# A float32 fast-multiplication kernel: turns for two engines in its planner, finer products as single steps, and two more products split

## Chip, cores and metric

One core of one Trainium2 chip. The metric is device time in microseconds (us), the median of several runs. Five engines matter: PE multiplies, DVE (VectorE) and POOL (GpSimd) add and subtract, ACT (ScalarE) copies, SP (SyncE) starts the transfers.

## What is computed

`x` is 64 sequences of 64 tokens with 1024 features, so 4096 tokens, all float32. Two residual layers follow each other. The first adds a low-rank product chosen by a sequence's adapter. The second adds a full 1024 x 1024 product and a mixture of eight low-rank experts, of which the two best by a router count, with a bias for the sequence's language.

```python
def _L0_cond_ref(x, A, B, adapter_ids):
    B_req = B[adapter_ids]
    A_req = A[adapter_ids]
    Bx = jnp.einsum('bni,bri->bnr', x, B_req)
    out = jnp.einsum('bnr,bor->bno', Bx, A_req)
    return out * SCALING
...
def _L1_cond_ref(x, language_ids, W, Wr, A, B):
    base = jnp.einsum('btd,od->bto', x, W)
    logits = jnp.einsum('btd,ed->bte', x.astype(jnp.float32), Wr.astype(jnp.float32))
    ...
    topw, topi = jax.lax.top_k(logits, TOP_K)
    weights = jax.nn.softmax(topw, axis=-1)
    gates = jnp.sum(jax.nn.one_hot(topi, E, dtype=weights.dtype) * weights[..., None], axis=-2)
    h = jnp.einsum('btd,erd->bter', x, A)
    lora_out = jnp.einsum('bter,bte,eor->bto', h, gates, B)
    return base + SCALING * lora_out
...
x = x + _L0_cond_ref(x, L0_cond_A, L0_cond_B, itok_B_4_50)
x = x + _L1_cond_ref(x, itok_B_0_7, L1_cond_W, L1_cond_Wr, L1_cond_A, L1_cond_B)
```

## The kernel before

**Tiling.** Tokens come in eight blocks of 512, held with features on the partitions. Two blocks make a stage `s`, so there are four stages, s = 0 to 3. The identity is added to the diagonal of W, so that the large product gives the residual too.

**Three levels of fast multiplication.** The large product of a stage is done with seven half-size products in place of eight (the outer level, `n`, in the order 1, 2, 6, 7, 5, 3, 4), and each of these with seven inner products (`k`, in the same order) in place of eight. An inner product is four matmuls of 128 x 128 weights with 256 tokens. From s = 1 (FINE, line 256) some inner products are split once more: `fine_product` (line 995) makes them of seven matmuls of 128 x 128 with 128 tokens. `fine_of` (line 669) says which: k = 2 for every n, and k = 4 for the n in FOURTH (line 257), except in the last product of the kernel. The last stage's last n keeps k = 2 alone.

**What a split product needs.** Sums of weight blocks (`fine_weights`, line 746): made in stage 1 by four instructions on POOL in one step, stored in `f_kept`, loaded again in stages 2 and 3. Sums of token blocks (`begin_fine`, line 979): three instructions on POOL in one step into a "tt" tile. Its matmuls go in four parts (`fine_product`, parts 0 to 3), one after each of the following whole products (`advance`, line 1163). After each of the first three parts ACT copies some of the sums in PSUM into a "cp" tile. After the last, DVE adds PSUM to the output (`leave`, line 951), and then `rest_` (line 1057) adds the copied pieces on POOL by three instructions in one step.

**Other work.** `turn`, `project` and `adapt` (lines 418 to 507) do the first layer for a block; `rows`, `gates` and `weigh` (lines 509 to 623) do the router. `inner_tokens` (line 800) makes four token sums for each n ("ti" tiles), on DVE in stage 0 and on POOL afterwards. `weights` (line 709) makes inner weight sums on POOL in stage 0, stores them in `s_kept`, and later loads seven of them for each n. `outer` and `token_sum` make the outer level's sums on DVE. A matmul of the gated rows with the expert weights ("extra", two for each product) joins the products with n and k in (2, 7, 3, 4).

**Who sets the order.** Every piece of work is a step given to `Plan` (line 34): engines that may do it with a cost in us, what it reads and writes, a due time `at`, buffers that it takes, and `sb` when all its operands lie in SBUF. `order` (line 65) walks through time: among the steps that could start soonest on an engine (within LOOK, 0.2 us) it takes the one with the earliest due time. If a DVE step and a POOL step with `sb` overlap, both are stretched by PACE (lines 145 to 152). The outcome is each engine's own list in program order (`Pinned`, line 19). On the chip every engine runs its list and waits for data and buffers alone.

**Buffers** (line 263). PSUM has two banks for "a" (pa, products 1, 6, 5, 3), two for "b" (pb, products 2, 7, 4 and the split k = 2) and four for "l", shared by turns, projections, rows and the split k = 4. An adaptation takes four "l" at a time (line 475). In SBUF "s" holds 27 tiles of weights, "tt" and "cp" three each.

In the profile all instructions issued through `Pinned` carry line 29, so one goes by the names: pf is a split product, tt its token sums, sf its weight sums, cp the copied pieces, u, v and o the sums that become the output, px an adaptation, pt and pg transposes, ph rows.

Of the kernel before, what the change touches and what calls it, by code (L numbers as in the profile page):

```python
# [33 lines left out]
class Plan:  # L34
# [14 lines left out]
    AHEAD = 6.0  # L49
    PACE = {"DVE": 0.36, "POOL": 0.73}  # L50
    SET = {"SP": 1.2, "DVE": 3.1, "POOL": 2.9}
# [13 lines left out]
    def order(self):  # L65
# [34 lines left out]
        turn = {tag: 0 for tag in turns}  # L100
        clock, end, where, now = dict(self.SET), {}, {}, {}
        moved = 0.0
        done = []
# [78 lines left out]
def kernel(  # L182
# [73 lines left out]
    FINE = 1  # L256
    FOURTH = (1, 2, 6, 7, 3)

# [212 lines left out]
    def adapt(k, h, at):  # L471
# [33 lines left out]
        for gi in range(NG):  # L505
            xs = part(x, gs=[gi])
            plan.add({"DVE": 0.62}, out(gi), [(px[gi],)] + xs, xs, at - 2 + 1.5 * gi * (k == 0))

# [157 lines left out]
    s_kept = tc.dram_tile([7, 7, P, QC * QO], F32, name="s_kept")  # L666
    f_kept = tc.dram_tile([7, 2, P, QC * QO], F32, name="f_kept")
# [16 lines left out]

    DVE = {"DVE": 0.62}
    POOL = {"POOL": 1.25}

    def outer(n, at):

        if n == 5:  # L690
            m_q[5] = {k: ("m5",) + k for k in quarter[1, 0]}
            for k in m_q[5]:
                combine(m_q[5][k], quarter[1, 0][k], quarter[1, 1][k], ALU.add, at, DVE)
        elif n == 7:
            m_q[7] = quarter[1, 0]
            for k in m_q[7]:
                combine(m_q[7][k], quarter[0, 0][k], m_q[7][k], ALU.subtract, at, DVE)
        elif n == 6:
            m_q[6] = quarter[0, 0]
            for k in m_q[6]:  # L700
                combine(m_q[6][k], m_q[5][k], m_q[6][k], ALU.subtract, at, DVE)
        elif n == 3:
            m_q[3] = quarter[0, 1]
            for k in m_q[3]:
                combine(m_q[3][k], m_q[3][k], m_q[6][k], ALU.subtract, at, DVE)

    wt, ti = {}, {}

    def weights(s, n, at):
# [17 lines left out]
        for k, (u, v, op) in {  # L727
# [7 lines left out]
            vv = m[v] if isinstance(v, tuple) else out[v]  # L735
            combine(out[k], uu, vv, op, at - 4, POOL)
        for k in ORDER:
# [8 lines left out]
    def fine_weights(s, n, k, a, at):  # L746

        t, kept = ("sf", s, n, k), f_kept[n - 1, k // 4]

        def blocks():  # L750
            made[t] = new("s", [P, QC, QO], f"sf_{s}_{n}{k}")
            return made[t].rearrange("p c (o w) -> p (c o) w", w=P)

# [3 lines left out]

        def sums(e):
            f, w4 = blocks(), made[a].rearrange("p c (o w) -> p (c o) w", w=P)
            a11, a21, a12, a22 = (w4[:, x] for x in range(4))  # L760
            v = engine[e]
            v.tensor_tensor(f[:, 0], a21, a22, ALU.add)
            v.tensor_tensor(f[:, 1], f[:, 0], a11, ALU.subtract)
            v.tensor_tensor(f[:, 2], a11, a21, ALU.subtract)
            v.tensor_tensor(f[:, 3], a12, f[:, 1], ALU.subtract)

# [3 lines left out]
        if s == FINE:  # L770
            plan.add({"POOL": 1.6}, sums, [(a,)], [(t,)], at - 3, [("s", t)], sb=True)
            plan.add({"SP": 0.1}, keep, [(t,)], [("fine", n, k)], at + 4, kb=256)
        else:
            plan.add({"SP": 0.1}, load, [("fine", n, k)], [(t,)], at - 6, [("s", t)], kb=256)
        wt[n]["fine", k] = t
# [24 lines left out]
    def inner_tokens(s, n, m, at):  # L800
# [7 lines left out]
        for k, u, v in ((5, (0, 1), (0, 0)), (6, (1, 1), 5), (7, (1, 1), (0, 1)), (4, (1, 0), 6)):  # L808
            t = ("ti", s, n, k)

            def fn(e, t=t, k=k, u=u, v=v):
# [5 lines left out]
            plan.add(  # L817
                POOL if s else DVE, fn, keys(*u) + vk, [(t,)], at - 5,
                [(f"t{k}", t)], sb=True,
# [39 lines left out]
    def products(s):  # L859
# [91 lines left out]
        def leave(n, ps, i, cs, js, more=False):  # L951
# [18 lines left out]
            if d == n and not fresh:  # L970
                reads.append((name(d, i), 0, 0))
            plan.add(
                {"ACT": 0.6} if src is None else DVE, fn, reads, qk(d, i, cs, js), at() - 4,
                [("o", name(d, i))] * fresh,
# [4 lines left out]
        def begin_fine(n, k):  # L979

            t, (tx, tk) = ("tt", s, n, k), ti[n][k]

            def fn(e):
                made[t] = new("tt", [P, 4, P], f"tt_{s}_{n}{k}")
                f, b, v = made[t], tx(), engine[e]
                b11, b21 = b[:, 0, :P], b[:, 1, :P]
                v.tensor_tensor(
                    f[:, :2], b[:, :, P:], b[:, 0, :].rearrange("p (h t) -> p h t", t=P), ALU.subtract
                )
                v.tensor_tensor(f[:, 2], f[:, 1], b11, ALU.add)  # L990
                v.tensor_tensor(f[:, 3], b21, f[:, 2], ALU.subtract)

            plan.add({"POOL": 1.7}, fn, tk, [(t,)], at() - 3, [("tt", t)], sb=True)

        def fine_product(n, k, part_):


            ps, cp, tag = ("pf", s, n, k), ("cp", s, n, k), "b" if k == 2 else "l"
            a, f, t, (tx, tk) = wt[n][k], wt[n]["fine", k], ("tt", s, n, k), ti[n][k]
            extra = hd[n][k] if n in (2, 3, 7, 4) and part_ == 3 else None  # L1000
            oh, row = {2: 0, 3: 0, 7: 1, 4: 1}.get(n), k // 4

# [28 lines left out]

            reads = [(a,), (f,), (t,)] + tk + ([("b1",), extra[1]] if extra is not None else [])
            plan.add(
# [14 lines left out]
            if part_ < 3:  # L1048
# [4 lines left out]
                return  # L1053
            leave(n, ps, row, ALL, (0,), True)
            region = qk(dest[n], row, ALL, (0,))

            def rest_(e):
                o, c, v = q(dest[n], row, ALL, (0,)), made[cp], engine[e]
# [6 lines left out]
            done(n, row, ALL, (0,))  # L1065

# [62 lines left out]
        def step(n, k):  # L1129
# [8 lines left out]
            if k in (1, 6, 5, 3):  # L1138
# [5 lines left out]
                if k == 5 and last(n):  # L1144
                    leave(n, ps, 0, ALL, (1,))
                if k == 5 and 4 in fine_of(s, n):
                    leave(n, ("pb2", s, n), 1, ALL, (0,), True)
# [24 lines left out]
        for n in ORDER:  # L1172
# [21 lines left out]
            else:  # L1194
# [113 lines left out]
```

## Time and profile before

| | us |
|---|---|
| median of 3 runs | 516.18 (515.77 to 516.62) |
| the profiled execution | 517.08 |
| its span, first to last instruction | 515.3 |
| granted TensorE clock | 0.999 |
| first matmul starts, last one ends | 9.8, 511.7 |
| PE busy between 59 and 511 | 451.97 of 452 |
| DVE busy, 59 to 183 (stage 0) | 95.5 of 124 |
| DVE busy, 183 to 249, 249 to 307 | 39.2 of 66, 37.3 of 58 |
| POOL busy, 59 to 183 | 72.9 of 124 |
| POOL busy, 183 to 249, 249 to 307 | 55.9 of 66, 38.2 of 58 |
| mean transfer rate | 211 GB/s |

The span is the stretch that the trace covers; the execution's time also has what lies around it. Busy time of a stretch is read engine by engine; an engine that is idle and for which nobody waits costs nothing. A matmul in float32 leaves two records in the trace, each shown longer than the distance to the next one, since matmuls are pipelined.

### The profile page before, as it was taken

Reading aid. Unit: us, or ns where it says so; the run is one execution under the profiler, and the core shown is the slowest. Engines: PE = TensorE matmul, PEld = TensorE weight load, DVE = VectorE, ACT = ScalarE, POOL = GpSimd, SP = SyncE. Lnnn points to the kernel's source line nnn. Section 1 sums busy time; section 2 is a strip of 40 time slices with the busy share of each in tenths; the row PEclk is TensorE's granted clock in tenths of the full one; section 3 lists DMA queues with packets and bytes.
Section 4 is the critical chain, followed back from the end, with each engine's and each line's share of the span. In section 5 each row is a group of like instructions: output and inputs, shape, how many; then the busy total and the mean of one; then the engine's idle time right before and its main releaser. Section 6 shows DMA issues by size and latency. Waiting matters only on the chain.

```text
span 515.3 us, 9478 instructions
## 1 busy us (share of the span) xinstructions
PE 501.1 (97%) x3648; PEld 441.6 (86%) x3648; DVE 329.3 (64%) x589; ACT 71.4 (14%) x189; POOL 318.7 (62%) x405
## 2 busy tenths in 40 slices
PE   2999999999999999999999999999999999999997
PEld 2857988889889998899888999889889899998986
DVE  0689998987975275536985456463878526742833
ACT  1111100001001130012110121102301111111110
POOL 3063058095467686997958557972954755997811
PEclk9999999999999999999999999999999999999999
DMA  7999185799585303999577633981855754581023
GB/s 260 371 354 369 67 280 211 256 332 317 176 261 206 90 15 101 335 342 350 173 253 248 211 131 118 380 281 43 284 176 190 246 149 134 169 270 41 38 98 111
DMA packets 59452, 108.69 MB, mean 211 GB/s; under 512 B 5520, under 2 KB 11664, under 8 KB 59408
## 3 DMA queue, kind: packets, MB, share of 16 engines
q1 hardware_dynamic: 57104, 99.70, 56.7%
q0 software_dynamic: 2304, 8.39, 4.8%
q8 instruction: 29, 0.48, 0.4%
q14 instruction: 15, 0.12, 0.1%
HBM read 75.30 MB, written 32.77 MB: 210 GB/s over the span
## 4 chain that ended last, share of the span: by engine, by line
PE 97%; DMA 2%; DVE 0%; issue 0%; SPq 0%; POOL 0%
PE pa L29 39%; PE pb L29 23%; PE pf L29 15%; PE ph L29 12%; PE px L29 3%; PE pw L29 3%; DMA x<-in_xT 2%; PE pt L29 1%; PE pg L29 1%; DVE o L29 0%; SPq L29 0%; DVE bx L29 0%; POOL x L29 0%
## 5 line engine op out<-in xcount | busy, mean ns | idle before, releaser
L29 PE MATMUL pa<-ti,s 128*128 128x256 f32 x432 | 102.0, 380 | 0.0
L29 PEld LDWEIGHTS pa<-ti,s 128*128 128x128 f32 x432 | 79.2, 190 | 9.8 <-issue 0.2
L29 PE MATMUL pb<-ti,s 128*128 128x256 f32 x264 | 65.6, 380 | 0.0
L29 PE MATMUL ph<-a_sb,x 128*128 128x136 f32 x512 | 62.8, 279 | 0.2 <-issue 0.2
L29 PEld LDWEIGHTS ph<-a_sb,x 128*128 128x128 f32 x512 | 61.8, 190 | 1.1 <-issue 0.4
L29 ACT COPY cp<-pf 128x128 f32<-128x128 f32 (+1 forms) x108 | 32.2, 302 | 201.0 <-PE pf L29 189.1
L29 PEld LDWEIGHTS pb<-ti,s 128*128 128x128 f32 x264 | 48.6, 190 | 5.9
L29 PE MATMUL pa<-x,s 128*128 128x256 f32 x216 | 52.4, 380 | 0.0
L29 POOL TENSOR_TENSOR ti<-x,ti 128x512 f32<-128x512 f32 x24 | 32.2, 1340 | 27.7 <-PE pf L29 22.6
L29 POOL TENSOR_TENSOR o<-o,cp 128x128 f32<-128x128 f32 (+1 forms) x54 | 34.5, 651 | 20.9 <-DVE o L29 15.6
L29 DVE TENSOR_TENSOR x<-px,x 128x512 f32<-128x512 f32 x64 | 39.8, 683 | 10.8 <-PE px L29 10.7
L29 PEld LDWEIGHTS pa<-x,s 128*128 128x128 f32 x216 | 39.4, 190 | 4.9 <-issue 0.2
L29 PE MATMUL pf<-tt,sf 128*128 128x128 f32 x216 | 42.1, 278 | 0.0
L29 POOL TENSOR_TENSOR ti<-t 128x512 f32<-128x512 f32 x18 | 23.3, 1294 | 29.3 <-PE pa L29 16.8
L29 POOL TENSOR_TENSOR ti<-x 128x512 f32<-128x512 f32 x24 | 31.0, 1292 | 16.7 <-PE pb L29 11.2
L29 PE MATMUL pa<-t,s 128*128 128x256 f32 x168 | 41.2, 380 | 0.0
L29 PEld LDWEIGHTS pf<-tt,sf 128*128 128x128 f32 x216 | 35.5, 191 | 3.2 <-issue 0.8
L29 DVE TENSOR_TENSOR o<-pa,u 128x512 f32<-128x512 f32 x32 | 22.0, 687 | 22.2 <-PE pa L29 11.2
L29 POOL TENSOR_TENSOR s<-w,w 128x512 f32<-128x512 f32 x12 | 17.1, 1428 | 29.1 <-PE pa L29 13.2
L29 POOL TENSOR_TENSOR ti<-t,ti 128x512 f32<-128x512 f32 x18 | 25.3, 1404 | 15.7 <-PE pf L29 12.2
L29 PEld LDWEIGHTS pa<-t,s 128*128 128x128 f32 x168 | 30.8, 190 | 3.9 <-issue 0.2
L29 DVE TENSOR_TENSOR o<-pb,o 128x512 f32<-128x512 f32 x35 | 23.6, 688 | 8.7 <-ACT o L29 4.6
(150 smaller groups left out, 850.9 us busy)
## 6 DMA issues: line engine op xcount, KB each, us to landing
s<-s_kept SPq DMA_DIRECT2D x147, 256.0 KB, 3.9
x<-in_xT SPq DMA_DIRECT2D x15, 1024.0 KB, 6.8
out_T<-o SPq DMA_DIRECT2D x30, 512.0 KB, 3.2
s_kept<-s SPq DMA_DIRECT2D x28, 256.0 KB, 4.6
sf<-f_kept SPq DMA_DIRECT2D x24, 256.0 KB, 2.8
s_kept<-w SPq DMA_DIRECT2D x18, 256.0 KB, 5.6
w<-in_w SPq DMA_DIRECT2D x16, 256.0 KB, 7.5
f_kept<-sf SPq DMA_DIRECT2D x12, 256.0 KB, 3.3
```

The costliest lines, as they stand in the source:

```text
L29: return self._tc.keep_in_program_order(f(*args, **kwargs))
```

## The change

The planner's stretch by PACE goes. In its place, a step with `sb` may start only when the last one with `sb`, on either engine, has ended; among engines that could start at the same time the one that was ready first goes first. Costs of several steps are raised a little (0.62 to 0.65 or 0.69, 1.25 to 1.3). FOURTH now names all seven n. A split k = 4 begins after product 6 instead of after 7, and the old order of what is left over (3, then 4) remains only for the n without a split k = 4. The sums of split products become steps of one instruction that may go to DVE or to POOL: four for weights, three for tokens, and two in place of three for the copied pieces. "s" gets 26 tiles, `f_kept` a third row. A new tuple THIRD (products with k = 3 split) is empty, so its branches do nothing.

```diff
@@ class Plan
-    PACE = {"DVE": 0.36, "POOL": 0.73}
...
-            return t
+
+            return (max(t, shared_), t) if st["sb"] else (t, t)
...
-            t0 = min(can[e])[0]
-            _, n, t = min((steps[n]["at"], n, t) for t, n in can[e] if t <= t0 + self.LOOK)
+            t0 = min(can[e])[0][0]
+            _, n, t = min((steps[n]["at"], n, t) for (t, _), n in can[e] if t <= t0 + self.LOOK)
...
-            other = {"DVE": "POOL", "POOL": "DVE"}.get(e)
-            if st["sb"] and other in now and clock[other] > t and steps[now[other]]["sb"]:
-
-                mine, theirs = st["eng"][e] / self.PACE[e], (clock[other] - t) / self.PACE[other]
-                both = min(mine, theirs)
-                clock[e] = t + both + (mine - both) * self.PACE[e]
-                clock[other] = t + both + (theirs - both) * self.PACE[other]
-                end[now[other]] = clock[other]
-            now[e] = n
+            if st["sb"]:
+                shared_ = clock[e]
...
-    FOURTH = (1, 2, 6, 7, 3)
+    FOURTH = (1, 2, 6, 7, 5, 3, 4)
+    THIRD = ()
...
-        "q": 7, "s": 27, "tt": 3, "cp": 3, "t5": 2, "t6": 2, "t7": 2, "t4": 2, "o": 3, "hg": 3, "hd": 3,
+        "q": 7, "s": 26, "tt": 3, "cp": 3, "t5": 2, "t6": 2, "t7": 2, "t4": 2, "o": 3, "hg": 3, "hd": 3,
...
-        return ((2, 4) if n in FOURTH and (s, n) != (NSUP - 1, ORDER[-1]) else (2,)) if s >= FINE else ()
+        if s < FINE:
+            return ()
+        if (s, n) == (NSUP - 1, ORDER[-1]):
+            return (2,)
+        return (2,) + (4,) * (n in FOURTH) + (3,) * (n in THIRD)
...
         if s == FINE:
-            plan.add({"POOL": 1.6}, sums, [(a,)], [(t,)], at - 3, [("s", t)], sb=True)
-            plan.add({"SP": 0.1}, keep, [(t,)], [("fine", n, k)], at + 4, kb=256)
+            for x in range(4):
+                plan.add(
+                    {"DVE": 0.29, "POOL": 0.48}, sums(x), [(a,)] + [(t, y) for y in range(x)], [(t, x)], at - 3,
+                    [("s", t)] * (x == 0), sb=True,
+                )
+            plan.add({"SP": 0.1}, keep, [(t, x) for x in range(4)], [("fine", n, k)], at + 4, kb=256)
...
-            plan.add({"POOL": 1.7}, fn, tk, [(t,)], at() - 3, [("tt", t)], sb=True)
+            for x, cost in enumerate(({"DVE": 0.42, "POOL": 0.75}, {"DVE": 0.29, "POOL": 0.48}, {"DVE": 0.29, "POOL": 0.48})):
+                plan.add(
+                    cost, sums(x), tk + [(t, y) for y in range(x)], [(t, x)], at() - 3,
+                    [("tt", t)] * (x == 0), sb=True,
+                )
...
-                c11, c21, c2 = o[:, 0, :P], o[:, 1, :P], o[:, 1]
-                v.tensor_tensor(c11, c11, c[:, 0], ALU.add)
-                v.tensor_tensor(c2, c2, c[:, 1:3].rearrange("p h t -> p (h t)"), ALU.add)
-                v.tensor_tensor(c21, c21, c[:, 3], ALU.add)
-
-            plan.add({"POOL": 1.7}, rest_, [(cp,)] + region, region, at() - 4, sb=True)
...
+                    o, c = (o[:, :, :P], c[:, 0::3]) if x == 0 else (o[:, 1].rearrange("p (h t) -> p h t", t=P), c[:, 1:3])
+                    v.tensor_tensor(o, o, c, ALU.add)
...
+            for x in range(2):
+                plan.add({"DVE": 0.42, "POOL": 0.75}, rest_(x), [(cp,)] + region, region, at() - 4, sb=True)
...
-                    if k == 7 and 4 in fine_of(s, n):
-                        going.append([n, 4, 0])
+                    if k in (6, 5) and k - 2 in fine_of(s, n):
+                        going.append([n, k - 2, 0])
                     advance()
-                if 4 in fine_of(s, n):
-                    rest = [(n, 3)]
-                    continue
+                rest = [(n, k) for k in (3, 4) if k not in fine_of(s, n)]
+                if last(n):
+                    rest = [(n, 4), (n, 3)]
+                continue
```

More of the change, by code (lines that the diff above doesn't have):

```diff
@@ L100, in order @@
         turn = {tag: 0 for tag in turns}
-        clock, end, where, now = dict(self.SET), {}, {}, {}
-        moved = 0.0
+        clock, end, where = dict(self.SET), {}, {}
+        moved = shared_ = 0.0
         done = []
@@ L506, in adapt @@
             xs = part(x, gs=[gi])
-            plan.add({"DVE": 0.62}, out(gi), [(px[gi],)] + xs, xs, at - 2 + 1.5 * gi * (k == 0))
+            plan.add({"DVE": 0.69}, out(gi), [(px[gi],)] + xs, xs, at - 2 + 1.5 * gi * (k == 0))
     def rows(k, at):
@@ L666 @@
     s_kept = tc.dram_tile([7, 7, P, QC * QO], F32, name="s_kept")
[L667 removed]
+    f_kept = tc.dram_tile([7, 3, P, QC * QO], F32, name="f_kept")
     def fine_of(s, n):
[L671 removed]
+        if s < FINE:
[3 more added lines that the diff above has]
+        return (2,) + (4,) * (n in FOURTH) + (3,) * (n in THIRD)
     def combine(out, a, b, op, at, engines):
@@ L683, in combine @@
         plan.add(engines, fn, [(a,), (b,)], [(out,)], at, [("s", out)] * fresh, sb=True)
-    DVE = {"DVE": 0.62}
-    POOL = {"POOL": 1.25}
+    DVE = {"DVE": 0.65}
     def outer(n, at):
@@ L692, in outer @@
             for k in m_q[5]:
-                combine(m_q[5][k], quarter[1, 0][k], quarter[1, 1][k], ALU.add, at, DVE)
+                combine(m_q[5][k], quarter[1, 0][k], quarter[1, 1][k], ALU.add, at, {"DVE": 0.65})
         elif n == 7:
@@ L696, in outer @@
             for k in m_q[7]:
-                combine(m_q[7][k], quarter[0, 0][k], m_q[7][k], ALU.subtract, at, DVE)
+                combine(m_q[7][k], quarter[0, 0][k], m_q[7][k], ALU.subtract, at, {"DVE": 0.65})
         elif n == 6:
@@ L700, in outer @@
             for k in m_q[6]:
-                combine(m_q[6][k], m_q[5][k], m_q[6][k], ALU.subtract, at, DVE)
+                combine(m_q[6][k], m_q[5][k], m_q[6][k], ALU.subtract, at, {"DVE": 0.65})
         elif n == 3:
@@ L704, in outer @@
             for k in m_q[3]:
-                combine(m_q[3][k], m_q[3][k], m_q[6][k], ALU.subtract, at, DVE)
+                combine(m_q[3][k], m_q[3][k], m_q[6][k], ALU.subtract, at, {"DVE": 0.65})
     wt, ti = {}, {}
@@ L735, in weights @@
             vv = m[v] if isinstance(v, tuple) else out[v]
-            combine(out[k], uu, vv, op, at - 4, POOL)
+            combine(out[k], uu, vv, op, at - 4, {"POOL": 1.3})
         for k in ORDER:
@@ L746, in fine_weights, with grid @@
     def fine_weights(s, n, k, a, at):
-        t, kept = ("sf", s, n, k), f_kept[n - 1, k // 4]
+        t, kept = ("sf", s, n, k), f_kept[n - 1, k - 2]
         def blocks():
             made[t] = new("s", [P, QC, QO], f"sf_{s}_{n}{k}")
-            return made[t].rearrange("p c (o w) -> p (c o) w", w=P)
+            return grid(made[t])
+        def grid(m):
+            return m.rearrange("p c (o w) -> p (c o) w", w=P)
         def load(e):
@@ L756, in load, with sums, fn @@
             sp.dma_start(made[t].rearrange("p c o -> p (c o)"), kept)
[L758 to L765, printed above, removed]
+        def sums(x):
+            def fn(e):
+                f, w4 = blocks() if x == 0 else grid(made[t]), grid(made[a])
+                a11, a21, a12, a22 = (w4[:, y] for y in range(4))
+                v = engine[e]
+                if x == 0:
+                    v.tensor_tensor(f[:, 0], a21, a22, ALU.add)
+                elif x == 1:
+                    v.tensor_tensor(f[:, 1], f[:, 0], a11, ALU.subtract)
+                elif x == 2:
+                    v.tensor_tensor(f[:, 2], a11, a21, ALU.subtract)
+                else:
+                    v.tensor_tensor(f[:, 3], a12, f[:, 1], ALU.subtract)
+            return fn
         def keep(e):
@@ L770, in fine_weights @@
         if s == FINE:
-            plan.add({"POOL": 1.6}, sums, [(a,)], [(t,)], at - 3, [("s", t)], sb=True)
-            plan.add({"SP": 0.1}, keep, [(t,)], [("fine", n, k)], at + 4, kb=256)
+            for x in range(4):
[4 more added lines that the diff above has]
+            plan.add({"SP": 0.1}, keep, [(t, x) for x in range(4)], [("fine", n, k)], at + 4, kb=256)
         else:
-            plan.add({"SP": 0.1}, load, [("fine", n, k)], [(t,)], at - 6, [("s", t)], kb=256)
+            plan.add({"SP": 0.1}, load, [("fine", n, k)], [(t, x) for x in range(4)], at - 6, [("s", t)], kb=256)
         wt[n]["fine", k] = t
@@ L817, in inner_tokens @@
             plan.add(
-                POOL if s else DVE, fn, keys(*u) + vk, [(t,)], at - 5,
+                {"POOL": 1.3} if s else DVE, fn, keys(*u) + vk, [(t,)], at - 5,
                 [(f"t{k}", t)], sb=True,
@@ L972, in leave @@
             plan.add(
-                {"ACT": 0.6} if src is None else DVE, fn, reads, qk(d, i, cs, js), at() - 4,
+                {"ACT": 0.6} if src is None else {"DVE": 0.69}, fn, reads, qk(d, i, cs, js), at() - 4,
                 [("o", name(d, i))] * fresh,
@@ L981, in begin_fine, with sums, fn @@
             t, (tx, tk) = ("tt", s, n, k), ti[n][k]
[L983 to L988, printed above, removed]
-                )
-                v.tensor_tensor(f[:, 2], f[:, 1], b11, ALU.add)
-                v.tensor_tensor(f[:, 3], b21, f[:, 2], ALU.subtract)
-            plan.add({"POOL": 1.7}, fn, tk, [(t,)], at() - 3, [("tt", t)], sb=True)
+            def sums(x):
+                def fn(e):
+                    if x == 0:
+                        made[t] = new("tt", [P, 4, P], f"tt_{s}_{n}{k}")
+                    f, b, v = made[t], tx(), engine[e]
+                    if x == 0:
+                        v.tensor_tensor(
+                            f[:, :2], b[:, :, P:], b[:, 0, :].rearrange("p (h t) -> p h t", t=P), ALU.subtract
+                        )
+                    elif x == 1:
+                        v.tensor_tensor(f[:, 2], f[:, 1], b[:, 0, :P], ALU.add)
+                    else:
+                        v.tensor_tensor(f[:, 3], b[:, 1, :P], f[:, 2], ALU.subtract)
+                return fn
+            for x, cost in enumerate(({"DVE": 0.42, "POOL": 0.75}, {"DVE": 0.29, "POOL": 0.48}, {"DVE": 0.29, "POOL": 0.48})):
+                plan.add(
+                    cost, sums(x), tk + [(t, y) for y in range(x)], [(t, x)], at() - 3,
+                    [("tt", t)] * (x == 0), sb=True,
+                )
         def fine_product(n, k, part_):
@@ L999, in fine_product @@
             a, f, t, (tx, tk) = wt[n][k], wt[n]["fine", k], ("tt", s, n, k), ti[n][k]
+            tts = [(t, x) for x in range(3)]
             extra = hd[n][k] if n in (2, 3, 7, 4) and part_ == 3 else None
-            oh, row = {2: 0, 3: 0, 7: 1, 4: 1}.get(n), k // 4
+            oh, row, js = {2: 0, 3: 0, 7: 1, 4: 1}.get(n), k // 4, (k % 2,)
             def fn(e):
@@ L1030, in fn @@
                         )
-            reads = [(a,), (f,), (t,)] + tk + ([("b1",), extra[1]] if extra is not None else [])
+            reads = [(a,)] + [(f, x) for x in range(4)] + tts + tk + ([("b1",), extra[1]] if extra is not None else [])
             plan.add(
@@ L1053, in fine_product, with rest_, fn @@
                 return
[L1054 to L1058, printed above, removed]
-                c11, c21, c2 = o[:, 0, :P], o[:, 1, :P], o[:, 1]
-                v.tensor_tensor(c11, c11, c[:, 0], ALU.add)
-                v.tensor_tensor(c2, c2, c[:, 1:3].rearrange("p h t -> p (h t)"), ALU.add)
-                v.tensor_tensor(c21, c21, c[:, 3], ALU.add)
-            plan.add({"POOL": 1.7}, rest_, [(cp,)] + region, region, at() - 4, sb=True)
-            done(n, row, ALL, (0,))
+            leave(n, ps, row, ALL, js, True)
+            region = qk(dest[n], row, ALL, js)
+            def rest_(x):
+                def fn(e):
+                    o, c, v = q(dest[n], row, ALL, js), made[cp], engine[e]
+                    o, c = (o[:, :, :P], c[:, 0::3]) if x == 0 else (o[:, 1].rearrange("p (h t) -> p h t", t=P), c[:, 1:3])
+                    v.tensor_tensor(o, o, c, ALU.add)
+                return fn
+            for x in range(2):
+                plan.add({"DVE": 0.42, "POOL": 0.75}, rest_(x), [(cp,)] + region, region, at() - 4, sb=True)
+            done(n, row, ALL, js)
         def done(n, i, cs, js):
@@ L1145, in step @@
                     leave(n, ps, 0, ALL, (1,))
+                if k == 5 and 3 in fine_of(s, n):
+                    leave(n, ps, 0, ALL, (1,))
                 if k == 5 and 4 in fine_of(s, n):
```

## The prediction

> **What bounds the kernel now.** The first view is the page's busy time and its slices, to see which engine has no room.
>
> ```profile
> PE 501.1 (97%) x3648; PEld 441.6 (86%) x3648; DVE 329.3 (64%) x589; ACT 71.4 (14%) x189; POOL 318.7 (62%) x405
> ...
> PE   2999999999999999999999999999999999999997
> ...
> PE 97%; DMA 2%; DVE 0%; issue 0%; SPq 0%; POOL 0%
> ```
>
> PE is full in 38 of 40 slices, and the chain that ended last (third line) is PE for 97% of the span. A busy PE could still hide waits, so the second view is PE's own list of waits, complete:
>
> ```profile
> PE pt L29 <- DMA gb<-in_b,idx: 9.8, 1, 9.8
> PE px L29 <- DVE bx L29: 0.4, 1, 0.4
> PE pb L29 <- DMA x<-in_xT: 0.2, 1, 0.2
> PE ph L29 <- issue: 0.2, 1, 0.2
> ```
>
> The columns are total us, times and longest. All four lie in the first 20 us, ahead of any line that the change touches except the planner. After that PE waits for nobody: 511.7 us is where its last matmul ends, and 3.6 us of last addition and last store follow. So only two things move the time: what PE is given to do, and whether PE begins to wait.
>
> The third view is the chain in order of time, where pieces of one kind stand alone and can be priced (start, us, what, records; a float32 matmul leaves two records):
>
> ```profile
> 224.61 0.89 PE pf L29 x8
> 225.50 1.73 PE pa L29 x8
> ...
> 229.08 0.22 PE pf L29 x2
> ```
>
> A whole inner product (four 128x256 matmuls) is 1.73 us. A split one is seven 128x128 matmuls: a first part of four (0.89) and three parts of one (0.22 each).
>
> The fourth view shows that DVE and POOL are led by PE and not the reverse, and how far ahead they work:
>
> ```profile
> POOL ti L29 <- PE pf L29: 34.8, 9, 7.0
> ...
> 308.03 0.45 POOL L29 TENSOR_TENSOR tt<-t,tt 128x128 f32<-128x128 f32 x1
> ...
> 315.00 0.39 PE L29 MATMUL pf<-tt,s 128*128 128x128 f32 x2
> ```
>
> The columns of the first line are as before: POOL's largest waits are for PE to give buffers back. The last two lines, from the timeline, are one product's finer token sums: done at 308.48, last of its four read at 315.00, the first a fifth of a us sooner. Matching all 36 split products in order, this lead is 3.0 us at the least and 13 us in the middle.
>
> **The change part by part.** *Two more products are split (line 257).* FOURTH gains n=5 (stages s=1, 2, 3) and n=4 (s=1, 2; the last product of the kernel is excepted, line 671): five products. Each takes 1.73 us off PE and puts 0.89 + 3 x 0.22 = 1.55 on it. From start to start the records are 112 ns apart, so 14 x 0.112 = 1.56 and a saving of 0.17. The two gate matmuls of n=4 are in either form. Five times 0.17 is **0.85 us**, all on the path. The bounds are 0.8 and 0.9 by the two readings.
>
> *Where the product enters (line 1207).* It now begins after product 6 rather than after 7, one whole product (1.73 us) sooner, for all n. The lead of 3 us at the least stays positive: 1.3 us. PE's work is the same, only interleaved otherwise. Interleaving has one price: the narrow 32-row and 32-column passes (px, pb of the next block) cost about 0.2 us at each entry and exit, since two halves of a projection apart took 1.01 each and joined 1.88, so 0.13 per cut. There are two joined and two cut pairs after 158 us. From -0.3 to +0.3 us; I take 0.
>
> *Fine sums become steps of one instruction for either engine.* The rows for the two engines, min/median/max in ns:
>
> ```profile
> L29 POOL TENSOR_TENSOR tt<-ti x15: 719/726/1053, 149.9 to 474.3; 128x256 f32<-128x256 f32 x15
> L29 POOL TENSOR_TENSOR tt<-tt,ti x15: 452/454/784, 151.0 to 475.1; 128x128 f32<-128x128 f32 x15
> ...
> L29 DVE TENSOR_TENSOR hd<-hg x8: 409/520/1015, 48.5 to 438.8; 128x256 f32<-128x256 f32 x8
> ...
> L29 DVE TENSOR_TENSOR w<-w,ident x8: 277/284/1352, 23.2 to 40.1; 128x128 f32<-128x128 f32 x8
> ```
>
> Undisturbed, DVE needs 0.41 and 0.28 us where POOL needs 0.73 and 0.45. There will be 41 split products (36 now). Per product, token sums are one wide and two narrow instructions: 0.97 on DVE, 1.63 on POOL. The additions of the copied parts become two wide ones instead of a wide and two narrow: 0.82 or 1.46, against 1.63 now. Weight sums, 14 times in s=1, are four narrow ones: 1.12 or 1.80. All on DVE: 41 x 1.79 + 14 x 1.12 = 89 us. All on POOL: 41 x 3.09 + 14 x 1.80 = 152 us, about what they cost POOL now (tt 67, sf 24, cp 65 us: 156). From 105 us to the end DVE is busy 246 of 406 us by the windows; with all 89 it would be 335, 82%. Neither end makes DVE or POOL the bound over a stage, so the price on PE is 0. What hides it is the lead above. If that cover is gone, a late token sum costs PE its lateness directly.
>
> *A new wait.* A token sum on DVE can stand waiting for a tt buffer, or for its first part made on POOL, and behind it in DVE's order are the additions that empty PSUM (o<-pa, u<-pa, o<-pf). The banks for pa are two, taken in turn by products that start some 14 to 18 us apart, and the drain of one ended at 323.91 while the bank's turn came near 334. A blocked DVE costs PE nothing below some 10 us. From 0 to several us; I take 0, since DVE idles a third of the time.
>
> *Turns.* The planner no longer lets two SBUF sums overlap in its reckoning and slows neither; it plans one after the other. It writes no semaphore for that: each engine still runs its own list and waits for data alone. So collisions will stay, fewer where the lists alternate. Now DVE's u<-u,o takes 679 ns at its fastest and 1138 in the mean, and POOL's ti 1264 and about 1330. Fewer collisions would save time on engines off the path: 0.
>
> The Trainium skill, "Perfetto Trace Analysis", section Optimizing Scalar/DVE Operations, speaks against this change: the two engines share an SBUF read port, so moving work from one to the other might not help. The rows just given agree that they disturb each other; by the rule alone the moved sums win nothing, and the total would still be that of the five products, because PE ends last. "SBUF — State Buffer", section Who interferes with whom, adds that whichever starts first holds the pair for its whole instruction; no list order alone prevents that here.
>
> *Transfers.* Two more stores of 256 KB in s=1, two more loads in s=2 and one in s=3, on SP's queue beside 147 + 24 such loads. One lands in 2.8 us and is asked for slots ahead. "s" has 26 buffers instead of 27, with 9 tiles for each n: two sets and eight tiles instead of three sets. A load lands in 3.9 us while an n lasts some 17. Price 0; if the queue's order turned bad, one load late is at most its 3.9 us.
>
> **Sum.** The profiled execution took 517.08 us with a span of 515.3, so 1.8 us lie around it; it was 0.9 above the median of the runs, 516.18. Less 0.85 it is 516.2, and by the median **515.3 us**, 0.16% less. Less than 0.2% is about what a measurement of this kernel can't tell from no change.
>
> **The rivals.** *A: PE stays fed and the time is 515.3.* Chance 0.70. For it: no PE wait in 490 us, PE-led waits on all others, spare time on DVE and POOL. Around 515.3 the medians of three runs scatter by some 0.4 (the three runs span 515.77 to 516.62), so 0.33 falls beyond 0.2% faster and 0.37 within.
>
> *B: the four "l" banks run short, slower.* Fourth products live in the same four banks as the next blocks' turns, projections and rows, and one adaptation (px) wants all four at once (line 475). Today n=5 and n=4 leave these banks free, at slots 28 to 35 and 42 to 49, just where the second next block is prepared (slots 32 to 37). If px is put off, the next stage's token sums come late, and PE waits at two seams (s=1 to 2, 2 to 3). A split product holds a bank for about 8 us (first part to drain); if what must wait for one has 6 us of margin, each seam costs 2 us: 515.3 + 4 = 519.3. It decides as soon as the planner finds no other PE work while px waits. Against it: x of that block is first needed some 12 slots, 30 us, later. Chance 0.24 with its like, such as DVE's drains coming late by over 10 us.
>
> *C: the turns do nothing on the chip.* The collisions stay as they are: u<-u,o again near 1138 ns. The five products still save 0.85, so 515.3; if collisions even grow, nothing reaches PE before the lead of 3 us is used up. It lies within A.
>
> *D: more is won.* The new order also joins the cut narrow passes and trims the 0.8 us of small early waits: 515.3 - 0.3 - 0.4 = 514.6. Against it: the early waits are for transfers that the change leaves alone. Chance 0.06, with all of it faster.
>
> **How the numbers follow.** The likeliest is A, 515.3; its own range is 514.7 to 516.0. B takes 0.24, and to leave no more than 2 in 10 outside I reach up to 518.6 and down to 514.6. Faster: 0.33 + 0.06, rounded to 0.38; within 0.2%: 0.37; slower: 0.25.
>
> **What would show it.** Right: PE's list of waits still ends at 20 us; matmul records near 3648 + 5 x 6 = 3678 (14 for 8 in each product); tt sums 123, some on DVE; DVE's share up and POOL's down by tens of us; the span down by 0.8. The mechanism is wrong if PE waits after 20 us, whatever the time: then its releaser names the step that failed, a PSUM drain on DVE, a px put off, a load, or a token sum. The prediction is wrong on size if PE's total falls by clearly other than 0.85 us.

## The result, and the profile after

The changed kernel takes **518.68 us** (518.18 to 521.15, 7 runs) where the kernel before takes 516.44 (515.77 to 516.62, 7 runs). The ratio is 1.0049, with a 95% interval of 1.0033 to 1.0064: slower by 2.2 us. The forecast of 515.3 had the wrong sign, and the range ended at 518.6. The profiled execution took 518.18 us with a span of 516.4.

The page of the changed kernel, busy time, slices and the chain of waits by engine:

```profile
PE 501.0 (97%) x3678; PEld 442.3 (86%) x3678; DVE 366.5 (71%) x700; ACT 75.8 (15%) x204; POOL 261.0 (51%) x296
...
PE   2999999999999999999999999999999999999997
...
DVE  0787998879776576766776775755877758673864
...
PE 93%; DMA 4%; DVE 3%; issue 0%; ACT 0%; SPq 0%; POOL 0%
```

The records of PE are the 3678 worked out, and POOL has given 58 us away. Nothing here looks 2 us slower. What has changed is the last line: the chain runs through DVE and DMA for 7%, where it was 97% PE.

The complete list of what PE waited for (total us, times, longest):

```profile
PE pt L29 <- DMA gb<-in_b,idx: 10.2, 1, 10.2
PE pa L29 <- DVE o L29: 0.8, 1, 0.8
PE px L29 <- DVE bx L29: 0.4, 1, 0.4
PE pf L29 <- ACT cp L29: 0.4, 1, 0.4
PE ph L29 <- issue: 0.2, 1, 0.2
```

Two lines are new and lie after 20 us: a drain on DVE (pa <- DVE o) and a copy on ACT (pf <- ACT cp). The chain shows what made the drain late (start us, us, what):

```profile
138.39 6.58 DMA out_T<-o
...
144.99 0.70 DVE o L29
...
145.74 1.99 PE pa L29 x8
```

A store of an output tile started at 138.39 and landed 6.58 us later. There are three such tiles, and DVE needed this one for the next drain. DVE's own row says how long it stood for it (timeline; in brackets the idle time before, and what ended it):

```profile
144.99 0.69 DVE L29 TENSOR_TENSOR o<-pa,u 128x512 f32<-128x512 f32 x1 [1.45 <-DMA out_T<-o]
```

DVE was held for 1.45 us, and PE waited 0.77 us for the PSUM bank behind it.

A third wait isn't in the list, since it lies inside a group of matmuls. From the timelines of PE and DVE (start us, us, what):

```profile
32.14 1.17 PE L29 MATMUL px<-bx,ga 32*128 32x128 f32 x32
...
36.87 2.27 PE L29 MATMUL px<-bx,ga 32*128 32x128 f32 x32
...
32.83 1.28 DVE L29 TENSOR_SCALAR den<-ex 128x4 f32<-128x4 f32 x1
...
35.45 2.48 DVE L29 TENSOR_TENSOR x<-px,x 128x512 f32<-128x512 f32 x4
```

The second adaptation takes 2.27 us where the first took 1.17: it begins at 36.87, while DVE, which did the router's small steps first (the row at 32.83 is one of them), is still emptying the first one's four banks. Before, that second adaptation began at 44.26.

**One measure free of the start and the last store.** The first 32 us scatter: the first group of 32 px records starts between 30.84 and 32.73 us in the kept profiles. From the start of that group (32.66 before) to the start of the last matmul, PE needs 478.46 us before and 480.39 after, 480.56 in a second execution. The table below calls this the path. Its growth in that second execution, by the distances between records (they come out up to 0.2 us longer than the idle times in the lists):

| | us |
|---|---|
| px at 37, banks not yet empty | +1.1 |
| drain at 145, output tile at its store | +0.8 |
| pf at 496, copied pieces not yet out of PSUM | +0.5 |
| a load of x at 218 | +0.3 |
| two more narrow passes cut in two | +0.2 |
| five products split | -0.8 |
| sum, beside 480.56 - 478.46 | 2.1, 2.1 |

### The profile page after: what moved, and what is told of

The parts are those of the page before. It is cut to its first block, busy times and chain, and to the rows that moved or that the text cites. A ratio compares the mean times of both kernels' runs of the same rounds, so it can differ in the third digit from the quotient of the medians.

```text
span 516.4 us, 9578 instructions
## 1 busy us (share of the span) xinstructions
PE 501.0 (97%) x3678; PEld 442.3 (86%) x3678; DVE 366.5 (71%) x700; ACT 75.8 (15%) x204; POOL 261.0 (51%) x296
## 4 chain that ended last, share of the span: by engine, by line
PE 93%; DMA 4%; DVE 3%; issue 0%; ACT 0%; SPq 0%; POOL 0%
PE pa L29 39%; PE pb L29 20%; PE pf L29 17%; PE ph L29 10%; PE px L29 3%; DMA x<-in_xT 2%; PE pw L29 1%; DMA out_T<-o 1%; PE pt L29 1%; PE pg L29 1%; DVE x L29 1%; DVE c L29 0%; DVE o L29 0%; DVE w L29 0%; DVE den L29 0%
## 5 line engine op out<-in xcount | busy, mean ns | idle before, releaser
L29 ACT COPY cp<-pf 128x128 f32<-128x128 f32 (+1 forms) x123 | 37.1, 303 | 190.4 <-PE pf L29 182.1
L29 PE MATMUL pb<-ti,s 128*128 128x256 f32 x224 | 55.9, 380 | 0.0
L29 PE MATMUL pf<-tt,sf 128*128 128x128 f32 x246 | 47.6, 277 | 0.4 <-ACT cp L29 0.4
L29 PEld LDWEIGHTS pf<-tt,sf 128*128 128x128 f32 x246 | 41.6, 191 | 4.5 <-ACT cp L29 0.5
L29 PEld LDWEIGHTS pb<-ti,s 128*128 128x128 f32 x224 | 40.9, 190 | 5.0 <-issue 0.4
L29 POOL TENSOR_TENSOR ti<-x,ti 128x512 f32<-128x512 f32 x24 | 31.1, 1296 | 8.7 <-PE pb L29 3.9
L29 POOL TENSOR_TENSOR o<-o,cp 128x256 f32<-128x256 f32 x29 | 23.4, 805 | 16.4 <-ACT cp L29 7.8
L29 POOL TENSOR_TENSOR ti<-t,ti 128x512 f32<-128x512 f32 x18 | 24.2, 1347 | 12.4 <-PE pf L29 11.8
L29 DVE TENSOR_TENSOR o<-pf,o 128x512 f32<-128x512 f32 x23 | 15.8, 687 | 16.9 <-PE pf L29 15.8
```

The costliest lines, as they stand in the source:

```text
L29: return self._tc.keep_in_program_order(f(*args, **kwargs))
```

## The experiments

Three theories were to be told apart. One: the saving on PE is there, and waits fixed in the new lists eat it, each because DVE has little room in stage 0. Two: the split products themselves cost more than they save, by interleaving or by banks. Three: the turns are a worse reckoning of what the chip does, and put DVE's steps where they come late. All runs, each with the ratio to the kernel before on the same chip:

| kernel | us | ratio, 95% | path, us |
|---|---|---|---|
| changed, again | 518.56 | 1.0043 (1.0030 to 1.0056) | 480.56 |
| changed, 4 output tiles, same lists | 518.77 | 1.0048 (1.0035 to 1.0061) | 483.74 |
| before, only the splits | 518.11 | 1.0034 (1.0021 to 1.0047) | 480.50 |
| changed, without the new splits | 519.39 | 1.0057 (1.0039 to 1.0075) | 481.58 |
| changed, px at 37 later | 518.61 | 1.0055 (1.0037 to 1.0073) | 480.31 |
| changed, 4 output tiles, 2 "hd" | 519.06 | 1.0055 (1.0034 to 1.0076) | 481.19 |
| both of these | 518.53 | 1.0047 (1.0029 to 1.0065) | 481.59 |
| before, 26 weight tiles | 516.01 | 0.9997 (0.9981 to 1.0012) | 478.43 |
| before, only the turns | 520.90 | 1.0075 (1.0051 to 1.0099) | 483.27 |
| changed, old reckoning | 518.34 | 1.0037 (1.0022 to 1.0052) | 480.86 |
| changed, flexible sums on POOL | 519.64 | 1.0073 (1.0050 to 1.0096) | 481.75 |
| before, 26 tiles, n=4 split | 515.51 | 0.9983 (0.9967 to 0.9998) | 478.10 |
| only the turns, one sum moved | 516.73 | 1.0012 (0.9996 to 1.0027) | 478.98 |
| changed, 4 output tiles, nothing shortened | 517.12 | 1.0011 (0.9999 to 1.0023) | 479.50 |
| the same, px at 37 later | 517.18 | 1.0024 (1.0011 to 1.0038) | 479.51 |

**1. The changed kernel again.**

> The changed kernel as it is, for a second profile. If its loss is PE waiting for PSUM drains that stand behind an output buffer whose store is late (late stores), the waits of PE after 20 us should fall at other places or have other lengths than the first profile's 0.9 us at 145 and 0.5 us at 495, and the span should follow their sum. If the loss is in the lists themselves (fixed waits), the same waits come back with the same lengths. Ratio to the kernel before near 1.004 by either.

The same three waits came at the same places: px at 37, the drain near 145 (0.6 us listed, 0.8 between records), and 0.35 for the copy at 496. They belong to the lists and not to the execution. A fourth, 0.22 for a load of x at 218, is in this execution alone.

**2. A fourth output tile, lists unchanged.**

```diff
+        n += {"o": 1, "s": -1}.get(tag, 0)
```

in the loop that makes the real buffers, after the plan.

> The planner's lists are those of the changed kernel, instruction for instruction; only the real buffers differ: four output tiles (o) in place of three, and 25 weight tiles in place of 26 to make room. Late stores: DVE no longer waits for out_T, the wait of PE at 145 us goes, and the time falls by 1 to 2.5 us, to a ratio of 1.000 or below. Fixed waits or moved sums (DVE's new sums hold up its drains): no change beyond 0.3 us, ratio 1.004.

The wait at 145 went, but with 25 weight tiles one of 0.8 us came at 174, so the time stayed. The profiled execution was the longest of its runs, 521.53 us, and shows something else (timeline, start us, us):

```profile
39.61 4.84 DVE L29 TENSOR_TENSOR h<-h,s 128x512 f32<-128x512 f32 x1
...
40.18 1.28 POOL L29 TENSOR_TENSOR s<-s,w 128x512 f32<-128x512 f32 x1
...
45.11 0.66 PE L29 MATMUL pg<-ident,h 128*128 128x128 f32 x4 [2.54 <-DVE x L29]
```

One DVE sum, 0.69 us in the profile of the changed kernel, took 4.84 beside sums on POOL, and PE waited 2.54 us for what is behind it. In the changed kernel's profile it began at 39.20 and was over before POOL's first sum at 40.72; here it was still running when that came at 40.18. Whether this is what makes the runs near 521 us is not shown: only this one was profiled.

**3. Only the splits, and everything but the splits.**

```diff
-    FOURTH = (1, 2, 6, 7, 3)
+    FOURTH = (1, 2, 6, 7, 5, 3, 4)
```

in the kernel before, and the reverse in the changed one.

> The kernel before with one edit: n = 5 and n = 4 split too (FOURTH as in the changed kernel). Nothing of the planner, the steps or the buffers changes. If the two further split products cost the time (banks l), this is slower than before by 1 to 3 us, ratio 1.003 to 1.006. If the planner's new lists cost it, PE's list of waits stays empty after 20 us and the time falls by 0.8 us, ratio 0.998.

> The changed kernel without the two further split products (FOURTH as before). Split products to blame: as fast as the kernel before, ratio 1.000. New lists to blame: slower than the changed kernel by the 0.85 us that the products save, or about its time, ratio 1.004 to 1.006, with waits of PE after 20 us.

Neither gives the loss to one side. With the old reckoning and POOL's steps of three instructions, the new splits alone lose 2.0 us on the path. Without them, the rest of the change loses 3.1. The first kernel's timeline at its largest wait (start us, us):

```profile
272.33 4.63 DVE L29 TENSOR_TENSOR t<-t,x 128x512 f32<-128x512 f32 x4
276.88 0.68 DVE L29 TENSOR_TENSOR o<-pa,v 128x512 f32<-128x512 f32 x1
...
277.62 1.56 PE L29 MATMUL pa<-ti,s 128*128 128x256 f32 x6 [0.98 <-DVE o L29]
```

Four DVE sums alternate with POOL's and take 4.63 us in place of 4 x 0.68; the drain queued behind them is late, and PE waits. Two more waits, 0.5 and 0.7 us between records, are for ACT's copies at 493 and 496. So a new list has waits of its own kind without the turns too.

**4. Mending px and the output tile, first attempts.** Px at 37 is exchanged with the next PE step by hand in the finished list (in `issue`, step 158 goes ahead of step 66); the fourth output tile is paid for with one "hd" tile.

```diff
+        for n, m in [(158, 66)]:
...
+        n += {"o": 1, "hd": -1}.get(tag, 0)
```

> The changed kernel's lists with one exchange on PE, by hand: the second adaptation of block 1 (px at 37 us) goes behind the next four pw matmul pairs (3.4 us) instead of ahead of them. Ledger theory (the loss is a few single waits that this order of lists makes): px takes 1.2 us again instead of 2.3, and the time falls by about 1.1 us, ratio near 1.002. If the loss is spread (DVE held up by moved sums everywhere), nothing changes: 1.0045.

> The changed kernel's lists, with four real output tiles instead of three and all 26 weight tiles kept (room from hd, two instead of three, and the gates' small tiles, one instead of two). Ledger theory: the wait of PE at 145 us (0.8 to 0.9) goes, since the drain no longer waits for the store, and no wait at 173 us comes, since that came with 25 weight tiles: the time falls by 0.8, ratio near 1.003. If the second look's 173 us wait comes again, it was not the weight tiles.

> Both edits of the two runs before. Ledger theory: the two waits add, 1.1 + 0.8 = 1.9 us less than the changed kernel, ratio 1.000 to 1.001; what is left is the wait for ACT near 495 us (0.5), narrow passes cut (0.25) and late x (0.3), against the 0.8 us that the split products save. Spread loss: no change, 1.0045.

None won time. In the first the wait left px, and pg waited 0.8 us at 41 instead, for a DVE drain: DVE is late for both, and this change of PE's order won nothing. In the second the wait at 145 went, and the tile taken away made a new one (timeline):

```profile
154.64 1.09 DVE L29 TENSOR_TENSOR hd<-hg 128x256 f32<-128x256 f32 x1 [4.56 <-PE pb L29]
...
160.32 0.92 PE L29 MATMUL pa<-ti,s 128*128 128x256 f32 x3 [1.48 <-DVE o L29]
```

DVE stood 4.56 us for one of two "hd" tiles, and the drain behind it came late. The experiment shows a queue behind a blocked DVE in stage 0, but not yet what the output tile is worth.

**5. Is any new list harmful, and do the turns do it?** One tile less in the kernel before makes another list. The new `order` alone makes another.

```diff
-        "q": 7, "s": 27,
+        "q": 7, "s": 26,
```

> The kernel before with 26 weight tiles instead of 27 and nothing else, so that the planner writes other lists from the same rules. If any new lists cost waits of this size (the lists of before being a lucky draw), this is slower by 0.5 to 2 us, ratio 1.001 to 1.004. If the loss belongs to the turns and the one-instruction steps, it stays within 1.000 +- 0.001.

> The kernel before with one edit: the new reckoning of SBUF steps (turns, no stretch). Products, steps and costs stay. Reckoning theory: the turns reserve for a DVE step of several small instructions only its undisturbed time (a gate step planned at 0.8 us takes 2.7 beside POOL), so lists are written on a DVE that is in truth late, and PE meets waits of 0.5 to 1.5 us at single places in stage 0: slower than the kernel before by 1 to 2 us, ratio 1.002 to 1.004. If only the moved and split steps cost time: ratio 1.000.

The first is as fast as before, with no wait after 20 us: the missing tile costs nothing, and neither does this new list. It is one draw and a mild one, since PE's order differs in only 202 of 3648 places. The turns alone lose 4.8 us on the path, the most of all and more than the 1 to 2 us expected. Where, the timeline shows (start us, us):

```profile
75.53 5.92 DVE L29 TENSOR_TENSOR x<-x,x 128x512 f32<-128x512 f32 x1
75.97 1.27 POOL L29 TENSOR_TENSOR s<-s,w 128x512 f32<-128x512 f32 x1
...
77.20 1.27 POOL L29 TENSOR_TENSOR s<-w,w 128x512 f32<-128x512 f32 x1
...
78.42 1.26 POOL L29 TENSOR_TENSOR s<-w,s 128x512 f32<-128x512 f32 x1
79.65 1.25 POOL L29 TENSOR_TENSOR s<-m,m 128x512 f32<-128x512 f32 x1
...
81.38 0.68 DVE L29 TENSOR_TENSOR u<-pa,u 128x512 f32<-128x512 f32 x1
...
82.20 3.20 PE L29 MATMUL pa<-t,s 128*128 128x256 f32 x8 [2.30 <-DVE u L29]
```

The DVE sum began 0.44 us ahead of POOL's chain of four sums and got through only when that had ended: 5.92 us, while POOL's sums kept their 1.27. In the planner's reckoning no two such sums overlap, so it had a turn of its own. Behind it the drain u<-pa,u was late, and PE waited 2.30 us. Then the matmuls themselves were slow (windows; us, then busy us and count of PE, PEld, DVE, ACT, POOL, then the granted clock, DMA share, GB/s):

```profile
79.00:82.00 3.00, 0.90 (x5) 0.45 (x3) 3.00 (x2) 0.00 (x0) 2.92 (x3) 1.00 0.74 288
82.00:86.00 4.00, 3.80 (x10) 3.12 (x11) 1.90 (x4) 0.00 (x0) 3.07 (x3) 0.60 0.45 175
86.00:95.00 9.00, 9.00 (x43) 7.89 (x42) 7.11 (x13) 0.00 (x0) 0.00 (x0) 0.99 0.46 147
```

In the 4 us around the end of the wait PE was granted 0.60 of its clock and was busy 3.80 us with 10 records, where the next window has 43 in 9: 10 should take 2.1 us, so some 1.7 more were lost. 2.3 and 1.7 are most of the 4.8.

**6. Moving that one sum.** In the list of the turns alone the DVE sum, step 115, goes ahead of step 226. In the timeline it then stands behind three of the drains that stood after it.

```diff
+        for n, m in [(115, 226)]:
```

> The kernel before with the turns alone (the run of 520.9 us) and one DVE step moved by hand: the sum x<-x,x that took 5.9 us beside a chain of POOL sums (75 us) goes behind the four drains that stood after it. Lockout theory: PE's wait of 2.5 us at 79.5 goes, and with it the 1.6 us of slower matmuls after it, so the time falls by about 4 us, to 517.0, ratio 1.002. If the loss is not this one wait, it stays near 520.9, ratio 1.0075.

The same place after it:

```profile
77.69 0.69 DVE L29 TENSOR_TENSOR u<-pa,u 128x512 f32<-128x512 f32 x1 [2.61 <-PE pa L29]
...
80.02 0.92 DVE L29 TENSOR_TENSOR x<-x,x 128x512 f32<-128x512 f32 x1
```

The sum takes 0.92, the wait is gone, the clock from 77 to 90 us is 1.00, and the path is 4.3 us shorter. One DVE instruction in the wrong place was nearly all that the turns alone had lost; what is left, 1.0012, can't be told from no change. One wait stays after 20 us, 0.3 for ACT's copy at 492.

**7. The turns or the flexible sums taken out of the change.** The changed kernel with the old `order` and PACE; and with its sums of one instruction on POOL alone:

```diff
-        {"DVE": 0.29, "POOL": 0.48}
+        {"POOL": 0.48}
...
-        {"DVE": 0.42, "POOL": 0.75}
+        {"POOL": 0.75}
```

> The changed kernel with the old reckoning (stretch by PACE) and everything else of the change. Reckoning theory: the waits at 37 and 145 us of the changed kernel go, so stage 0 is as before; but with one-instruction steps for both engines the old rule writes yet other lists, and waits from the two further split products (as in the kernel before with them alone, 2.4 us) stay: 1.003 or above. If the turns were harmless, as slow as the changed kernel, 1.0045, with the same waits in stage 0.

> The changed kernel with all steps of the fine sums on POOL alone (DVE taken from their list of engines). If sums moved to DVE hold up its drains, the time falls towards the kernel before, by 1 us or more. Reckoning theory: stage 0 is nearly the same list as in the changed kernel, so the waits at 37 and 145 us come back; ratio 1.004 or above.

With the old reckoning the waits at 37 and 145 go, so these two places do come from the turns. Others of the same kind come in: DVE's drains are late at 63, 79 and 94 (0.5, 0.2 and 0.6 us), ACT's copies twice. The path is no shorter. With the sums on POOL alone it is 1.2 to 1.4 us longer than with the choice, and the waits at 36 and 145 are still there: taking the sums from DVE wins nothing. But this list differs too, with waits of its own (0.9 at 244 for a DVE sum, 0.5 at 210 for a load of x), so it isn't a price of the moved sums.

**8. The output tile paid for elsewhere.** The room comes from single buffers for small tiles and from two tiles that share one; weights and "hd" keep all of theirs, and the lists stay.

```diff
+        n += tag == "o"
...
-tc.tile_pool(name="small", bufs=2)
+tc.tile_pool(name="small", bufs=1)
```

> The changed kernel's lists with four real output tiles, all 26 weight tiles and all three hd tiles (room from the gates' small tiles, one each instead of two, and from the language ids, which share the bias tile). If the buffer is what PE waits for at 145 us, and the waits at 173 and 158 us of the two earlier tries came from the room taken: no wait at 145, 158 or 173, 0.8 us less than the changed kernel, 517.8, ratio 1.003. If a wait comes again near 150 to 175 us, DVE is late there whatever the buffer, ratio 1.0045.

> As the run before, and px of block 1 behind four pw pairs on PE (the exchange tried alone before, where the wait went to pg, 0.9 us instead of 1.1). Expected 0.2 to 0.3 us below that run, 517.5; a fall by 1.1 would mean that the pg wait was chance.

The first kernel's timeline at the place of the wait, and then its complete list of PE's waits:

```profile
142.65 0.68 DVE L29 TENSOR_TENSOR o<-pa,u 128x512 f32<-128x512 f32 x1
```

```profile
PE pt L29 <- DMA gb<-in_b,idx: 9.3, 1, 9.3
PE px L29 <- DVE bx L29: 0.4, 1, 0.4
PE pf L29 <- ACT cp L29: 0.4, 1, 0.4
PE ph L29 <- issue: 0.3, 1, 0.3
```

The drain no longer stands for a store, the wait for it is gone, and the path is 0.9 to 1.1 us shorter, the median 1.4 to 1.6 (against the two measurements of the changed kernel, on other chips; the ratios fall from 1.0043 and 1.0049 to 1.0011). The path's part is near the 0.8 expected; the rest of the median's fall is not explained. What is left over the kernel before, 1.0 us of path, is px at 37 (1.1), the copy near the end (0.5) and the cut passes (0.2), less the 0.8 saved. Exchanging px wins nothing here either: pg waits 0.8 at 42 instead, and the path is the same. So no run here removes this largest wait without making another.

**9. Can the splits win?** The kernel before, 26 weight tiles, n=4 added and n=5 left whole:

```diff
-    FOURTH = (1, 2, 6, 7, 3)
+    FOURTH = (1, 2, 6, 7, 3, 4)
```

> The kernel before with 26 weight tiles and n = 4 split as well (two more split products, not five: n = 5 stays whole). Its lists are those of the run with 26 tiles, which had no waits, as long as n = 4 leaves enough whole products between the parts. Then it saves 2 x 0.17 = 0.33 us against that run, ratio 0.9993, hard to tell from none; if n = 4 makes waits as n = 5 did, above 1.001.

The page and PE's complete waits:

```profile
PE 500.8 (97%) x3660; PEld 441.8 (86%) x3660; DVE 330.5 (64%) x591; ACT 73.2 (14%) x195; POOL 329.1 (64%) x421
```

```profile
PE pt L29 <- DMA gb<-in_b,idx: 9.2, 1, 9.2
PE px L29 <- DVE bx L29: 0.4, 1, 0.4
PE pb L29 <- DMA x<-in_xT: 0.2, 1, 0.2
PE ph L29 <- issue: 0.2, 1, 0.2
```

Two more splits, 12 more records, no new wait: the path is 0.33 us shorter than with 26 tiles alone, beside the 2 x 0.17 worked out. At 515.51 us this is the lowest median of all, barely: the interval ends at 0.9998, the ratio is lower than the 0.33 us account for, and one of fifteen runs may come out so by chance.

Of the three theories the second falls in its general form, since here two more splits win their 0.33 on the path. The third is a part only: the old reckoning takes the waits at 37 and 145 away, and others come. The first stands, but what eats the saving isn't in stage 0 and behind DVE alone.

## Why the prediction was wrong, step by step

**Five products at 0.17 each: right.** 3678 records, 0.80 us less between undisturbed matmuls, and 0.33 for two of them where nothing waits.

**Where the product enters: right in size.** The lead of the token sums is 2.9 us at the least, which was put at 1.3, and no wait is for one. The narrow passes cost +0.2 within the -0.3 to +0.3.

**Fine sums on DVE at no cost: right for their own stages.** DVE went from 329 to 367 us and POOL from 319 to 261. From 183 to 307 us DVE is busy 88.7 of 124 us, and PE waits for it nowhere there. The kernel that keeps them on POOL is slower. The Trainium skill, "Perfetto Trace Analysis", section Optimizing Scalar/DVE Operations, says that such a move might not help. Here the kernels with the move stand at 1.0043 and 1.0049 and the one without at 1.0073, but their lists differ too, so no run isolates the move.

**"A new wait ... I take 0": this step failed.** Its margin, "a blocked DVE costs PE nothing below some 10 us", was read at one place in stage 2 and carried to the whole kernel, with the mean "DVE idles a third of the time" behind it. The timelines of the kernel before, there and in stage 0:

```profile
323.22 0.69 DVE L29 TENSOR_TENSOR o<-pa,u 128x512 f32<-128x512 f32 x1 [0.27 <-PE pa L29]
...
326.74 1.89 PE L29 MATMUL pa<-ti,s 128*128 128x256 f32 x8
329.79 1.99 PE L29 MATMUL pa<-t,s 128*128 128x256 f32 x8
```

```profile
65.91 0.68 DVE L29 TENSOR_TENSOR o<-pa,u 128x512 f32<-128x512 f32 x1
...
63.27 1.89 PE L29 MATMUL pa<-ti,s 128*128 128x256 f32 x8
65.00 1.89 PE L29 MATMUL pa<-t,w 128*128 128x256 f32 x8
66.74 1.10 PE L29 MATMUL pa<-x,s 128*128 128x256 f32 x4
```

Products take the two "pa" banks in turn. After the drain that ended at 323.91 the bank's next product is the second one, at 329.79 and not near 334: 5.9 us, not 10. In stage 0 the product at 63.27 is drained until 66.59 and its bank is taken again at 66.74: 0.15 us. So the kernel before had no wait and hardly any room, which a list of waits doesn't show. In the changed kernel a DVE held for 1.45 us at 145 cost PE 0.77, and with the turns alone one held for 5.92 cost 2.30. The step also looked for the blocked DVE in the wrong place, at token sums and "tt" tiles. What held it in the changed kernel was an output tile at its store (145) and the router's steps ahead of px (37); in two of the other kernels it was sums behind POOL's chains. The loss lies between the step's own ends, "0 to several us"; the value taken of the two was the wrong one.

**"Turns ... 0": failed with it.** That collisions stay was right, as rival C said; the group of the changed kernel, mean ns 1138 before:

```profile
L29 DVE TENSOR_TENSOR u<-u,o 128x512 f32<-128x512 f32 x16 | 17.6, 1103 | 0.8 <-POOL o L29 0.7
```

But the reckoning alone was priced as if it could only save. The list planned without the stretch put DVE's drains behind a sum that took 5.92 us, and nearly all of what the turns alone lost went with one sum moved.

**Transfers at 0: wrong in one place.** Not the loads that were counted but a store, 6.58 us to land, with only three tiles to cover it.

**The copies: not priced.** Near the end of the changed kernel two parts of split products follow one another with no whole product between, and the second waits for ACT's copy, 0.5 us between records:

```profile
495.27 0.38 PE L29 MATMUL pf<-tt,sf 128*128 128x128 f32 x2
496.00 0.49 PE L29 MATMUL pf<-tt,sf 128*128 128x128 f32 x2 [0.35 <-ACT cp L29]
```

The turns alone have such a wait too (0.3 at 497), without any new split, so which part of the change makes it is open.

**Rivals.** B had the sign and nearly the size (519.3 against 518.68), by luck. Its mechanism was split products that hold the "l" banks until PE waits at two seams. At 37 an adaptation does want four banks at once, but stage 0 has no split products: the adaptation before it holds them. No wait of the list lies at a seam. A and D fell.

**What stays open.** The waits of the changed kernel are accounted for, and the one at 145 was taken away by an experiment; the one at 37 wasn't. Why a given list has 2 to 3 us of them and another none isn't shown: of the lists of before and its variants three have none after 20 us, and those with the splits, the turns or the whole change nearly all have some. That the old list is among the lucky ones because it was chosen for its time is an argument, not something these runs show. The flexible steps alone, with neither turns nor splits, were not tried.

## What to carry to other kernels

When a kernel has an engine that never waits, an edit that redraws the order of the others is not priced by their idle time: it is priced by the smallest margin anywhere, here 0.15 us where 10 was assumed, so read the margin in the fullest stage and behind each scarce buffer. A planner's model of two engines that share something is judged by the longest instruction it failed to foresee, not by the mean. After such a redraw, list every wait of the bound engine and mend the two or three places; here one moved sum was worth 4.3 us and one more tile some 1 to 1.6, against 0.8 for the change itself.

## What was not expected of the hardware

A DVE sum with both inputs in SBUF that meets back-to-back sums on POOL can be kept out for the whole chain and not for one instruction: 5.92, 4.84 and 3.28 us where 0.68 is the undisturbed time, with POOL's at 1.25 to 1.29 throughout. The first two are shown above; in both the DVE sum began first, by 0.44 and 0.57 us, and was kept out all the same. The third is in the changed kernel, where PE didn't wait for it, and it comes again in its second execution (3.27):

```profile
116.14 3.28 DVE L29 TENSOR_TENSOR u<-u,o 128x512 f32<-128x512 f32 x1
```

Elsewhere the two alternate at some 1.7 us for POOL's and 1.2 for DVE's (272 us, only the splits). Which of the two happens wasn't settled. The Trainium skill, "SBUF — State Buffer", section Who interferes with whom, has the two engines contend for such a sum, and says of the two-port modes that whoever issues first holds the shared pair for the whole instruction. The chains measured here are longer than one instruction, and the sum that began first lost.

The granted clock fell to 0.60 for 4 us after one wait of 2.3 us, in the kernel with the turns alone, and stayed at 1.00 from 45 to 50 us after a wait of 2.5 us in the kernel of experiment 2. So a wait can cost nearly twice itself (2.3 and 1.7), but not always.
